# Decoder block on one core: score tiles split in two, and feed forward kept out of the weighted-values stages

## The chip, the cores and the metric

The kernel runs on one core of a Trainium2 chip. A core has a matrix engine (TensorE, PE in the profile, whose weight loads are listed as PEld), a vector engine (VectorE, DVE), an activation engine (ScalarE, ACT), a general engine (GpSimd, POOL) and a queue engine (SyncE, SP) that issues transfers here. Each engine takes its instructions in order. Two memories on the core matter: SBUF, which all engines read, and PSUM, eight banks of 128 partitions x 512 float32 numbers, into which TensorE writes. The metric is the device time of the one launch in microseconds, lower is better.

## The reference

Two sequences of 1024 tokens, 256 channels, 16 heads of 16 channels. Causal self attention, cross attention on a context of 77 tokens, and a gated feed forward with two hidden layers of 1024, each followed by a residual sum and a layer norm:

```python
x = _layernorm(x + attn(x, w_qkv, w_proj))            # causal, rotary, 16 heads
x = _layernorm(x + xattn(x, ctx, ctx, mask, Wq, ...)) # 77 keys
h = silu(x @ w1.T * w1_s) * (x @ w2.T * w2_s)
h = gelu(h @ h1.T * h1_s)
h = gelu(h @ h2.T * h2_s)
x = _layernorm(x + h @ w3.T * w3_s)
```

## The kernel before

The tokens are cut into five chunks (`CHUNKS`): two of 2 tiles of 128 tokens, then three of 4 tiles. For each chunk the attention work is a generator that goes through these stages:

- `start` (`project`): queries, keys and values, turned by the rotary tables.
- `top` (`maxima`): scores of each query tile against all keys that it sees, only to take the largest of each row. The scores of four heads stand in one PSUM tile `su` of four banks (`scores_bank`, L113), one head in each; one VectorE reduction (`part`, L432) takes the maxima of all four. The maxima are then added to the queries as a 17th row, so that later scores come out shifted.
- `weighted` (`values`, with `weights_and_values`): for each group of four heads and each key tile, TensorE writes the scores S into `su` (keys on partitions, up to 512 queries of four heads, 4 x 512 numbers for each partition), ScalarE takes the exponential into `pr` (L495), GpSimd clears what lies above the diagonal (L498), and TensorE sums the weighted values W of the step before into `po`.
- `rest` (`finish`, `cross`, `finish`): the division and projection, and the same for the cross attention, with its own maxima (`top`) and four steps of weighted values of 77 keys.

PSUM is full: `su` takes four banks and there is one such tile, `po` one, and three single banks serve everything else. So the scores of the next step cannot be written until the exponential (or the reduction) of this step has read all of `su`.

The feed forward of a chunk is a second generator (`fed`, `feed_forward_exact`). It works with bfloat16 products: each float32 operand is split into three bfloat16 parts, whose weights fit one bfloat16 exactly. It can begin once the attention of its chunk is done. `beside` (L861) weaves the two: each attention step yields a number of microseconds, its credit, and feed forward steps are drawn until the credit is spent. A step of the maxima yields 2.6 for 512 keys (L442), a step of weighted values 1.4 for 512 queries (L474), self and cross alike. From L940 on the engines keep the order of the program (`in_order`), so what is drawn at a yield stands on TensorE's queue between two attention steps. When the filler has run out or cannot go on, it yields nothing, and the attention steps stand alone; what is left of it after the attention is done runs by itself (L874). Attention runs in the order: `top(1)`, `weighted(1)`, then `rest(1)` woven with `start(2)` and `top(2)`, `weighted(2)`, and so on to `rest(4)`; the feed forward of the last chunk follows alone. Before all that, a first part without the fixed order does the attention of chunk 0 and surveys the weights (L820).

The functions that the change touches:

Of the kernel before, what the change touches and what calls it, by code (L numbers as in the profile page):

```python
# [9 lines left out]
F32 = mybir.dt.float32  # L10
# [28 lines left out]
def kernel(ctx: ExitStack, tc: tile.TileContext, a: dict, out: bass.AP):  # L39
# [73 lines left out]
    def scores_bank(name="su"):  # L113
        return pl.ps_u.tile([P, 4, 512], F32, tag="u", name=name)
# [205 lines left out]

    phase = [""]
# [75 lines left out]
    def maxima(b, t0, n, q):  # L397

        late = None
        for i in range(n):  # L400
# [3 lines left out]
            for m, (kk, c0, c1) in enumerate(spans):  # L404
                diagonal = m == len(spans) - 1
                r = c1 - c0
                gs = 512 // r
                for g0 in range(0, NG, gs):
                    gm = min(gs, NG - g0)
                    su = scores_bank()  # L410
                    calls = []
                    if diagonal:
                        for j in range(4):
                            to = su[:, j, :].rearrange("p (g n) -> p g n", g=NG)
                            mask = causal.unsqueeze(1).to_broadcast([P, NG, P])
                            calls.append(((to, ident_h, mask), dict(start=True, stop=False)))
                    for gi in range(gm):
                        for j in range(4):
                            rows = slice(32 * j, 32 * j + D)
                            calls.append(  # L420
                                (
                                    (
                                        su[:, j, gi * r : (gi + 1) * r],
                                        q[rows, g0 + gi, cols],
                                        kT[b, kk][rows, g0 + gi, c0:c1],
                                    ),
                                    dict(start=not diagonal, stop=(not diagonal or gi == gm - 1)),
                                )
                            )
                    tiled(calls)  # L430
                    turned = turned_maxima(m_pad) if late else None
                    dve.tensor_reduce(  # L432
                        part[:, m, g0 : g0 + gm, :].rearrange("p g j -> p j g"),
                        su[:, :, : gm * r].rearrange("p j (g r) -> p j g r", g=gm),
                        AX.X,
                        ALU.max,
                    )
                    if late:
                        add_maxima(turned, q, late)
                        late = None  # L440
                    phase[0] = "maxima"
                    yield 2.6 * gm * r / KB  # L442
# [7 lines left out]
    def weights_and_values(n, steps, q):  # L450
# [5 lines left out]
        def weigh(g, first, last, pr, heads, q0):  # L456
            if first:
                po[0] = pl.ps_o.tile([P, n * P], F32, tag="o", name="po")
            tiled(
                ((po[0][32 * j : 32 * j + 32, q0:], heads(j), pr[:, j, q0:]), dict(start=first, stop=last))  # L460
# [5 lines left out]
        for g, first, last, scores, weights, heads, q0 in steps:  # L466
# [7 lines left out]
            yield 1.4 * (n * P - q0) / KB  # L474
# [4 lines left out]
    def values(b, t0, n, q):  # L479
# [3 lines left out]
        def step(g, k):  # L483
# [3 lines left out]
            def scores(su):  # L487
                for j in range(4):
                    rows = slice(32 * j, 32 * j + D + 1)
                    key = kT[b, k // KT][rows, g, at * P : (at + 1) * P]  # L490
                    yield (su[:, j, q0 : n * P], key, q[rows, g, q0:]), dict(start=True, stop=True)

            def weights(su):
                pr = pl.probs.tile([P, 4, n * P], F32, tag="pr", name="pr")
                act.activation(pr[:, :, q0:], su[:, :, q0 : n * P], AF.Exp)  # L495
                if k >= t0:

                    nc.gpsimd.affine_select(  # L498
                        out=pr[:, :, q0 : q0 + P],
                        in_=pr[:, :, q0 : q0 + P],  # L500
                        compare_op=ALU.is_ge,
                        fill=0.0,
                        base=0,
                        pattern=[[0, 4], [1, P]],
                        channel_multiplier=-1,
                    )
# [7 lines left out]
        yield from weights_and_values(n, [step(g, k) for g in range(NG) for k in range(nk)], q)  # L514


    def cross(b, t0, n, qx):
# [8 lines left out]
        for i in range(n):  # L526
# [3 lines left out]
            for j in range(4):  # L530
                to = su[:, j, : NG * L].rearrange("p (g l) -> p g l", g=NG)
                mask = maskq[:, t0 + i, :].unsqueeze(1).to_broadcast([P, NG, L])
                calls.append(((to, ident_h, mask), dict(start=True, stop=False)))
            for g in range(NG):
                for j in range(4):
# [3 lines left out]
                            (su[:, j, g * L : (g + 1) * L], qx[rows, g, cols], kx[b][rows, g, :]),  # L539
# [6 lines left out]
            dve.tensor_reduce(  # L546
                top.rearrange("p g j -> p j g"),
                su[:, :, : NG * L].rearrange("p j (g l) -> p j g l", g=NG),
                AX.X,
                ALU.max,  # L550
            )
# [11 lines left out]
        def step(g):  # L563
            def scores(su):
                mask = maskk[:, t0 * P : (t0 + n) * P]
                for j in range(4):
                    yield (su[:L, j, : n * P], ident_h[:L, :L], mask), dict(start=True, stop=False)
                for j in range(4):
                    rows = slice(32 * j, 32 * j + D + 1)
                    yield (su[:L, j, : n * P], kx[b][rows, g, :], qx[rows, g, :]), dict(start=False, stop=True)  # L570

            def weights(su):
                pr = pl.probs.tile([P, 4, n * P], F32, tag="pr", name="pr")
                act.activation(pr[:L], su[:L, :, : n * P], AF.Exp)
                return pr[:L]
# [3 lines left out]
        yield from weights_and_values(n, [step(g) for g in range(NG)], qx)  # L579
# [281 lines left out]
    def beside(work, filler):  # L861
# [4 lines left out]
        for step in work:  # L866
            credit += step + stepped()
            while credit > 0:
                credit -= next(filler, None) or credit
            yield step  # L870
        attending[0] = False
# [64 lines left out]
    def beside_each_other(forward, wbufs):  # L936
        attended.clear()
# [103 lines left out]
```

## Time and profile before

| what | value |
|---|---|
| median of 3 runs | 1352.59 us (1347.74 to 1359.89) |
| the profiled execution | 1358.01 us, its span 1356.0 us |
| TensorE busy, mean granted clock | 1168.7 us, 0.861 |
| maxima, reduction of 4 x 512 numbers | 2291 ns each, 60 of the 76 |
| weighted values, exponential of 4 x 512 numbers | 1877 ns, 44 times |
| table loads of ScalarE | 27, 1283 ns each |

The stages lie in the span as follows, read from the first and last products of each tile: the first part to 143 us; `top(1)` to 179; `weighted(1)` to 217; `rest(1)`, `start(2)`, `top(2)` to 357; `weighted(2)` to 407; the same for chunk 3 to 644 and 763, for chunk 4 to 1009 and 1129; `rest(4)` to 1221; the last feed forward to the end.

A row of the busy time by stage gives the stretch in microseconds and its length, then for each engine the busy time and the number of instructions, then the granted clock of TensorE (1.00 is full speed), the share of the transfer engines and GB/s. A row of the timeline gives start, duration, engine, line, operation, the tile written and the tiles read, the shapes, and in brackets the idle time before it and what ended it. All attention and feed forward instructions are recorded through one helper, so their line is L81; they are told apart by their tiles: `su`, `pr`, `po` for attention, `pg`, `pu`, `pf` for feed forward. A float32 product counts as two instructions, so four heads are x8.

### The profile page before, as it was taken

What the parts mean: (1) busy time and instruction counts of PE and PEld (TensorE: products, weight loads), DVE (VectorE), ACT (ScalarE), POOL (GpSimd) and SP (SyncE); (2) the same over time, 40 slices, a digit from 0 to 9 for tenths busy, and PEclk for the clock granted to TensorE, in tenths of its full rate; (3) what the DMA queues carried; (4) which work ended last, traced back from release to release, by engine and by line L of the source; (5) the groups of instructions that cost most, each with busy time, mean ns of one, the idle gap of its engine ahead of it and who ended that gap; (6) DMA issues with size and microseconds to landing.
All of it is one profiled execution on the core that took longest, in us unless ns stands there. A gap on an engine that the chain in (4) does not pass through costs nothing.

```text
span 1356.0 us, 17661 instructions
## 1 busy us (share of the span) xinstructions
PE 1168.7 (86%) x7602; PEld 576.5 (43%) x7602; DVE 573.3 (42%) x868; ACT 395.6 (29%) x477; POOL 204.4 (15%) x262
## 2 busy tenths in 40 slices
PE   5878799987999768789898977788999988788997
PEld 3545456745546423334222454153332224433444
DVE  6442733436525434776212264157652024435112
ACT  4431243311352211112454320202134453223221
POOL 2010112111132100211202120002012021102221
PEclk7575899957999956899998996559998989969999
DMA  8740111110111000011000000000110000101110
GB/s 314 231 144 1 32 48 40 40 32 24 49 38 37 27 16 1 16 31 32 16 24 16 16 14 26 0 0 24 31 32 8 24 24 16 32 0 32 47 54 27
DMA packets 30952, 54.91 MB, mean 40 GB/s; under 512 B 5032, under 2 KB 10257, under 8 KB 30865
## 3 DMA queue, kind: packets, MB, share of 16 engines
q1 hardware_dynamic: 30593, 52.91, 12.6%
q8 instruction: 61, 1.00, 0.3%
q10 hardware_dynamic: 272, 0.79, 0.2%
q14 instruction: 26, 0.21, 0.0%
HBM read 45.82 MB, written 7.86 MB: 40 GB/s over the span
## 4 chain that ended last, share of the span: by engine, by line
PE 68%; DVE 18%; ACT 8%; POOL 2%; DMA 2%; issue 2%; SPq 0%; DVEq 0%; ACTq 0%; POOLq 0%
PE pf L81 24%; PE su L81 20%; PE pm L81 7%; DVE part L81 7%; PE po L81 6%; PE pt L81 5%; ACT pr L81 3%; DVE left L81 2%; PE pu L81 2%; PE pq L81 2%; DMA w<-in_wf_dram 2%; DVE gate L81 1%; DVE x L81 1%; PE pg L81 1%; DVE top L81 1%
## 5 line engine op out<-in xcount | busy, mean ns | idle before, releaser
L81 PEld LDWEIGHTS <-wf 128*128 128x128 bf16 x2400 | 224.3, 99 | 310.3 <-issue 150.5
L81 ACT ACTIVATE pr<-su 128x2048 f32<-128x2048 f32 (+3 forms) x124 | 171.2, 1381 | 231.9 <-PE su L81 230.2
L81 DVE TENSOR_REDUCE part<-su 128x4 f32<-128x2048 f32 (+3 forms) x76 | 165.6, 2179 | 85.9 <-PE su L81 85.4
L81 PE MATMUL pf<-mid,wf 128*128 128x512 bf16 (+1 forms) x640 | 171.2, 351 | 0.9 <-ACT v L81 0.7
L81 PE MATMUL pf<-hid,wf 128*128 128x512 bf16 (+1 forms) x640 | 166.7, 344 | 0.0
L81 PE MATMUL su<-q,kT 17*128 17x512 f32 (+3 forms) x832 | 101.0, 555 | 10.5 <-ACT pr L81 9.4
L81 PE MATMUL su<-kT,q 16*128 16x128 f32 (+3 forms) x1152 | 100.8, 463 | 8.1 <-DVE top L81 2.7
L81 PE MATMUL pf<-midm,wf 128*128 128x512 bf16 (+1 forms) x320 | 105.4, 342 | 1.2 <-ACT midm L81 1.1
L81 DVE COPY q<-po 128x512 f32<-128x512 f32 (+1 forms) x40 | 23.4, 585 | 195.0 <-PE po L81 195.0
L81 PE MATMUL pf<-hidm,wf 128*128 128x512 bf16 (+1 forms) x320 | 105.3, 337 | 0.0
L81 PE MATMUL po<-pr,v 128*32 128x512 f32 (+3 forms) x832 | 88.4, 500 | 14.7 <-POOL pr L498 14.6
L707 POOL TENSOR_TENSOR hid<-left 128x512 bf16<-128x512 f32 (+1 forms) x70 | 62.0, 891 | 215.4 <-DVE left L81 199.4
L498 POOL TENSOR_SCALAR_AFFINE_SELECT pr<-pr 128x512 f32<-128x512 f32 x64 | 42.6, 665 | 328.9 <-ACT pr L81 328.8
L81 ACT COPY hidm<-left 128x512 bf16<-128x512 bf16 (+1 forms) x70 | 36.3, 527 | 147.6 <-DVE left L81 147.6
L81 DVE TENSOR_TENSOR left<-hid 128x512 f32<-128x512 f32 (+1 forms) x80 | 51.6, 656 | 63.1 <-ACT hid L81 55.0
L81 PE MATMUL pu<-xTc,wf 128*128 128x512 bf16 (+1 forms) x160 | 50.9, 373 | 24.6 <-DVE gate L81 24.6
L81 PEld LDWEIGHTS su<-kT,q 16*128 16x128 f32 x1152 | 50.0, 219 | 45.1 <-issue 19.1
L81 PE MATMUL pg<-xTc,wf 128*128 128x512 bf16 (+1 forms) x160 | 51.7, 374 | 11.5 <-DVE q L81 7.5
L81 ACT ACT_TABLE_LOAD x27 | 34.6, 1283 | 88.2 <-PE su L81 87.9
L81 PEld LDWEIGHTS <-ident_h 128*128 128x128 bf16 (+1 forms) x208 | 26.4, 129 | 75.3 <-issue 67.1
L237 POOL TENSOR_SCALAR rstd<-mv 128x4 f32<-128x4 f32 (+1 forms) x15 | 3.4, 226 | 362.6 <-DVE mv L81 362.6
L81 PEld LDWEIGHTS su<-q,kT 17*128 17x128 f32 x832 | 35.8, 198 | 50.7 <-ACT pr L81 30.2
(125 smaller groups left out, 1403.4 us busy)
## 6 DMA issues: line engine op xcount, KB each, us to landing
wf<-wh SPq DMA_DIRECT2D x110, 256.0 KB, 2.6
w<-in_wf_dram SPq DMA_DIRECT2D x22, 512.0 KB, 5.5
wh<-h SPq DMA_DIRECT2D x22, 256.0 KB, 2.8
x<-in_x_dram SPq DMA_DIRECT2D x16, 128.0 KB, 3.1
out_dram<-x SPq DMA_DIRECT2D x16, 128.0 KB, 1.8
wqkv<-in_w_qkv_dram ACTq DMA_DIRECT2D x1, 768.0 KB, 4.4
wk<-in_wkT_dram SPq DMA_DIRECT2D x1, 512.0 KB, 7.3
wq<-in_wqT_dram SPq DMA_DIRECT2D x1, 512.0 KB, 4.9
```

The source lines that it names most:

```text
L81: ins = getattr(self.engine, name)(*args, **kw).ins
L237: nc.gpsimd.tensor_scalar(rstd, mv[:, :, 1], EPS, None, ALU.add)
L498: nc.gpsimd.affine_select(out=pr[:, :, q0 : q0 + P], in_=pr[:, :, q0 : q0 + P], compare_op=ALU.is_ge, fill=0.0, base=0, pattern=[[0, 4], [ ...
L707: nc.gpsimd.tensor_tensor(lower[:, k, :], left[:, 0, :], left_upper, ALU.subtract)
```

## The change

The scores of four heads become two tiles of two banks each, with a tag of their own, so each half is free on its own. For weighted values a new function `exponentials` lets VectorE copy the second half to SBUF while ScalarE takes the exponential of the first, then ScalarE takes that of the copy in place. The selection on GpSimd is done once for each half. For maxima a new function `largest` makes two reductions, one for each half; when feed forward has run out (`starving`), ScalarE first copies the second half to SBUF and the second reduction reads the copy. A step of weighted values of self attention yields 0.0 instead of 1.4, of cross attention 0.4; a step of the maxima yields 1.6 while starving and 2.6 otherwise. `beside` sets `starving` from what the filler answered.

```diff
     def scores_bank(name="su"):
-        return pl.ps_u.tile([P, 4, 512], F32, tag="u", name=name)
+        return [pl.ps_u.tile([P, 2, 512], F32, tag=f"u{i}", name=name) for i in range(2)]
...
+    def exponentials(su, p, cols):
+        n = cols.stop - cols.start
+        halves = [pl.probs.tile([P, 2, n], F32, tag=f"pr{i}", name=f"pr{i}")[:p] for i in range(2)]
+        dve.tensor_copy(halves[1], su[1][:p, :, cols])
+        act.activation(halves[0], su[0][:p, :, cols], AF.Exp)
+        act.activation(halves[1], halves[1], AF.Exp)
+        return halves
+
+    def largest(to, su, groups, r):
+        first, other = (t[:, :, : groups * r].rearrange("p j (g r) -> p j g r", g=groups) for t in su)
+        if starving[0]:
+            aside = pl.probs.tile([P, 2, KB], F32, tag="pr1", name="aside")[:, :, : groups * r]
+            aside = aside.rearrange("p j (g r) -> p j g r", g=groups)
+            act.copy(aside, other)
+            other = aside
+        dve.tensor_reduce(to[:, :2], first, AX.X, ALU.max)
+        dve.tensor_reduce(to[:, 2:], other, AX.X, ALU.max)
+
+    starving = [True]
...
-                    dve.tensor_reduce(
-                        part[:, m, g0 : g0 + gm, :].rearrange("p g j -> p j g"),
-                        su[:, :, : gm * r].rearrange("p j (g r) -> p j g r", g=gm),
-                        AX.X,
-                        ALU.max,
-                    )
+                    largest(part[:, m, g0 : g0 + gm, :].rearrange("p g j -> p j g"), su, gm, r)
...
-                    yield 2.6 * gm * r / KB
+                    yield (1.6 if starving[0] else 2.6) * gm * r / KB
...
-    def weights_and_values(n, steps, q):
+    def weights_and_values(n, steps, q, fill):
...
-            yield 1.4 * (n * P - q0) / KB
+            yield fill * (n * P - q0) / KB
...
-                pr = pl.probs.tile([P, 4, n * P], F32, tag="pr", name="pr")
-                act.activation(pr[:, :, q0:], su[:, :, q0 : n * P], AF.Exp)
+                pr = exponentials(su, P, slice(q0, n * P))
                 if k >= t0:
-                    nc.gpsimd.affine_select(
...
+                    for half in pr:
+                        nc.gpsimd.affine_select(
...
-        yield from weights_and_values(n, [step(g, k) for g in range(NG) for k in range(nk)], q)
+        yield from weights_and_values(n, [step(g, k) for g in range(NG) for k in range(nk)], q, 0.0)
...
-        yield from weights_and_values(n, [step(g) for g in range(NG)], qx)
+        yield from weights_and_values(n, [step(g) for g in range(NG)], qx, 0.4)
...
             while credit > 0:
-                credit -= next(filler, None) or credit
+                took = next(filler, None)
+                starving[0] = took is None
+                credit -= took or credit
             yield step
-        attending[0] = False
+        attending[0] = starving[0] = False
...
     def beside_each_other(forward, wbufs):
+        starving[0] = True
```

## The prediction

> **What bounds the kernel now.** I read the page first (engines, slices with the granted clock), then busy time by stage, then the groups with their shapes apart, then the order of time inside one step. TensorE is busy 1168.7 of 1356.0 us, but its granted clock is the second half of the story:
>
> ```profile
> PE 1168.7 (86%) x7602; PEld 576.5 (43%) x7602; DVE 573.3 (42%) x868; ACT 395.6 (29%) x477; POOL 204.4 (15%) x262
> PEclk7575899957999956899998996559998989969999
> ...
> core 0: us, PE busy (x) PEld busy (x) DVE busy (x) ACT busy (x) POOL busy (x), PEclk, DMA share, GB/s
> 179.00:217.00 38.00, 36.02 (x400) 19.96 (x400) 8.25 (x20) 20.67 (x22) 7.70 (x12) 1.00 0.15 41
> 287.00:309.00 22.00, 16.80 (x100) 10.79 (x98) 12.66 (x27) 0.75 (x2) 1.87 (x4) 0.50 0.11 34
> 357.00:407.00 50.00, 45.47 (x427) 22.88 (x426) 13.23 (x27) 27.04 (x22) 15.41 (x24) 0.97 0.13 39
> 407.00:466.00 59.00, 52.12 (x343) 36.23 (x341) 26.62 (x58) 15.70 (x31) 11.58 (x14) 1.00 0.11 32
> 466.00:546.00 80.00, 58.97 (x348) 27.13 (x347) 33.93 (x56) 10.26 (x9) 2.21 (x4) 0.64 0.04 10
> 644.00:763.00 119.00, 110.03 (x712) 32.77 (x710) 22.53 (x29) 58.77 (x38) 19.81 (x24) 0.94 0.07 18
> 821.00:910.00 89.00, 69.53 (x370) 33.09 (x369) 32.12 (x47) 10.95 (x10) 1.25 (x2) 0.53 0.02 5
> 1009.00:1129.00 120.00, 110.99 (x710) 32.55 (x709) 22.22 (x29) 58.77 (x38) 19.80 (x24) 0.93 0.06 18
> 1178.00:1204.00 26.00, 21.37 (x86) 5.07 (x87) 5.71 (x13) 8.77 (x5) 1.27 (x2) 0.62 0.12 37
> 1204.00:1221.00 17.00, 13.85 (x57) 9.31 (x56) 9.58 (x27) 1.49 (x4) 1.25 (x2) 0.80 0.00 0
> 1221.00:1356.00 135.00, 120.09 (x576) 55.63 (x574) 36.73 (x63) 32.95 (x51) 28.71 (x28) 0.97 0.13 40
> ```
>
> Weighted values are the rows at 179, 357, 644 and 1009 (327 us). The rows at 287, 466, 821, 1178 and 1204 (234 us) are stretches in which feed forward has run out: TensorE is busy about three quarters of them at nearly half clock. Now the inside of a step, and rows without feed forward:
>
> ```profile
> 706.17 1.14 PE L81 MATMUL su<-q,kT 17*128 17x512 f32 x8 [0.26 <-ACT pr L81]
> 707.24 1.06 PE L81 MATMUL po<-pr,v 128*32 128x512 f32 x8
> 707.44 1.88 ACT L81 ACTIVATE pr<-su 128x2048 f32<-128x2048 f32 x1 [1.32 <-PE su L81]
> 708.24 0.63 PE L81 MATMUL pf<-mid,wf 128*128 128x512 bf16 x2
> ...
> 885.00:905.00 20.00, 19.78 (x83) 12.69 (x84) 7.59 (x18) 1.49 (x4) 0.00 (x0) 0.50 0.00 1
> 1185.00:1203.00 18.00, 16.70 (x65) 3.20 (x64) 2.08 (x3) 5.62 (x3) 0.00 (x0) 0.50 0.03 8
> ```
>
> A step is scores (S), exponentials and the previous step's weighted values (W), with feed forward filling TensorE during the 1.88 us exponential. The last two rows have no feed forward: TensorE is busy 99% and 93% of them and stays at 0.50.
>
> **Where feed forward goes.** I counted its products between the stages in the instruction order of both programs, at 0.217 us for 512 columns (92 in each 20 us of 1260 to 1300). Total 458.3 us in both. The four stages of weighted values lose 15.4, 18.9, 43.0 and 43.0 and keep under 1 each. The stretches between gain 6.3 (217 to 357), 27.7 (407 to 644), 31.7 (763 to 1009) and 4.0 (1129 to 1204). What stands after the last attention work of the values kind grows from 114.6 to 162.7, so 48.1 of it is new there.
>
> **Weighted values, at full clock.** The scores tile is freed by halves: the exponential of a half is 1.02 us (the 128x1024 form, 1023 ns); a VectorE copy of 1024 numbers is not in the trace: at least 0.69 (512 numbers), and by the step from 425 ns (256) to 692 ns (512) it is 1.23, which I take as nearer in kind. Then S 1.14 and 0.19 of hand-over (0.06 from ScalarE to TensorE at 498.59, 0.13 back at 707.31): 2.56 us. W (1.00) lies beside the other exponential, and ScalarE's own 2 x 1.02 is under it. Narrower steps by the same sum: 2.1 (384), 1.6 (256), 1.5 for 128, where two selections on GpSimd take the place of one of 0.63. Each stage starts with a bare wait of 2.7 us: table load 1.28, exponential, hand-over, now with no product to cover it. A long stage has 20 full steps and 4 of each narrow width: 51 + 20.8 + 2.7 = 74.5; the stage at 357 has 4 full ones: 34; the one at 179 has 12 of 256 and 4 of 128: 28. Sum 211 against 327: -116.
>
> **Weighted values, at half clock.** Then TensorE's S and W bound the step: 2.00 and 1.94 in the cross steps at 1185 (matmul rows at 1185.31 and 1187.24), 3.94 in all. From the first stage of the program: 1.24 + 1.08 for 256, 0.81 + 0.66 for 128, 3.1 for 384 between them. 20 x 3.94 + 4 x (3.1 + 2.3 + 1.45) + 2.7 = 109; 46 and 36 for the shorter ones. Sum 300: -27 only, for 120 us of feed forward that has to be done elsewhere.
>
> Which clock? Every fall in the trace follows two to three microseconds with little TensorE work (the clock is 0.50 from 475 after a wait of 2.7 us). The start of each values stage now has such a wait, so I expect a fall in most. The way back is slow without feed forward: 46 to 73 is 26.50 of 27 us busy at 0.50, then it rises at 75. I take half of the stage at each clock: 255, **-72** (-116 to -27).
>
> [...]
>
> **The stretches between.** Starved work at full clock is busy time times clock: 8.4, 37.7, 36.9, 13.2 and 11.1 us. With filler TensorE is 88% busy (row at 407), so 9.5, 42.8, 41.9, 15.0, 12.6; plus the feed forward gained (6.3, 27.7, 31.7, 4.0 and some 8 in the last finish) that is 16, 70.5, 73.6 and 39.6 in place of 22, 80, 89 and 43: -34. But the four cross steps of a stage get only 0.4 of credit each; at half clock they cost 5.8 each (1185.31, 1191.18, 1197.03) instead of 2.9, 35 us over three long stages: 0. I take the middle, **-17**.
>
> **The end.** 48.1 less 8 is 40 us of feed forward alone, at 120.09 / 114.6 = 1.05: 42, and one layer boundary with no attention to cover gelu (1.91) and splitting: 5. **+47**. Nothing hides it.
>
> **Small terms.** Maxima now take two reductions: 1536 numbers take 1756 ns and 2048 take 2291, so 0.15 us more per pair. Some 50 pairs stand on VectorE in the stages; where filler covers them nothing, on the path 8; but the first half is free earlier, so perhaps a gain of 4: +3. Returning to feed forward at half clock, 4 x 1.5: +6 (0 to 12). ScalarE's aside copies appear twice in the branch that runs: nothing. First stage to 143 us, reordered by the scheduler: 0 (-5 to +8).
>
> **Sum.** 1356 - 72 - 17 + 47 + 9 = 1323 of span. The profiled run was 1358.0 at span 1356.0, the median 1352.6, so 3 off: **1319**.
>
> **Rivals.**
> Full clock in values and cross: -116 - 34 + 47 + 3 = -100, 1253. [...] Against: the bare 2.7 us at each start. Chance 0.17.
> Half clock throughout: -27 + 0 + 47 + 15 = +35, **1388**, slower. Place: TensorE's S and W in the values stages. It decides from the point where about three quarters of values and cross run at half clock (100 / 135). For it: the rows at 885 and 1185. Against: the rises at 75, 533 and 1208 without feed forward. Chance 0.25.
> The change does less than it says: if VectorE and ScalarE do not work side by side on the two tiles, a step is 1.02 + 1.23 + 1.14 + 0.19 = 3.6 at full clock, near the 3.5 of now but without filler: about 60 us over the full steps, 1375. They share no queue, so 0.05, within the slower case's bounds.
> The mixed case, my forecast: 0.53, itself 1285 to 1352.
>
> **How the numbers follow.** About 1% (13.5 us) is what a measurement tells from no change. Faster: the full-clock case and four fifths of the mixed one, 0.60; same: the upper end of the mixed and the low end of the half-clock one, 0.20; slower 0.20. Range 1258 to 1382, which leaves a tenth at each end.
>
> **What would show it.** In the after profile: clock in the values stages (0.5 or 1.0), a full step of 2.6 or 3.9 us, no stretch of 20 us without products of feed forward before the end, and some 160 us of feed forward alone at the end instead of 120. Wrong would be: starved stretches that remain, a step over 4 us, or maxima that lengthen although their filler is the same.

## The result, and the profile after

The changed kernel took 1405.9 us (median of 4 runs, 1400.99 to 1421.36) against 1350.16 us of the kernel before (4 runs beside it): a ratio of 1.042, 95% interval 1.032 to 1.053. It is slower; the forecast was 1319. The profiled execution took 1401.64 us, with a span of 1399.9 us.

First the page of the changed kernel: engines, the granted clock in 40 slices, and groups of instructions (busy us, mean ns, then idle time before).

```profile
PE 1240.9 (89%) x7602; PEld 589.0 (42%) x7602; DVE 663.9 (47%) x1044; ACT 429.0 (31%) x636; POOL 215.4 (15%) x326
PEclk8585889987899877998858997989955596999998
L81 PE MATMUL su<-q,kT 17*128 17x512 f32 (+3 forms) x832 | 151.7, 749 | 16.9 <-ACT pr L81 12.8
L81 PE MATMUL po<-pr,v 128*32 128x512 f32 (+3 forms) x832 | 146.0, 711 | 0.7
```

TensorE runs the same 7602 instructions and is busy for 72 us more. The two groups of the weighted values, scores and sums, on the page of the kernel before:

```profile
L81 PE MATMUL su<-q,kT 17*128 17x512 f32 (+3 forms) x832 | 101.0, 555 | 10.5 <-ACT pr L81 9.4
L81 PE MATMUL po<-pr,v 128*32 128x512 f32 (+3 forms) x832 | 88.4, 500 | 14.7 <-POOL pr L498 14.6
```

In the changed kernel they take 108 us more for the same products. The mean clock fell from 0.861 to 0.834, but that is only about half of it: in e16 below, where these stages run at 1.00, 0.87, 1.00 and 0.96, the two groups still take 124.7 and 115.3 us, 58 us less than here. The rest goes with the halves, whose products stand further apart: at full clock the scores of a full step spread over 1.58 us (678.58 below, clock 1.00 from 678 to 694), against 1.14 in the step at 706.17 of the kernel before (1.00 from 706 to 709). Busy time by stage of the changed kernel, columns as before:

```profile
core 0: us, PE busy (x) PEld busy (x) DVE busy (x) ACT busy (x) POOL busy (x), PEclk, DMA share, GB/s
181.00:211.00 30.00, 28.15 (x263) 12.15 (x261) 11.58 (x21) 17.89 (x33) 6.41 (x16) 0.78 0.04 10
...
355.00:394.00 39.00, 34.45 (x258) 10.84 (x257) 16.26 (x23) 24.13 (x34) 13.50 (x33) 0.82 0.03 8
...
476.00:507.00 31.00, 29.11 (x131) 9.71 (x130) 9.47 (x11) 12.29 (x12) 0.00 (x0) 0.61 0.06 17
507.00:552.00 45.00, 37.50 (x242) 24.35 (x240) 26.23 (x57) 7.63 (x17) 9.86 (x14) 0.82 0.16 47
...
649.00:746.00 97.00, 93.60 (x515) 23.06 (x515) 35.04 (x36) 55.69 (x64) 12.97 (x32) 0.64 0.00 1
1010.00:1119.00 109.00, 105.38 (x516) 24.07 (x517) 35.87 (x37) 58.24 (x67) 14.89 (x34) 0.52 0.00 1
...
1190.00:1400.00 210.00, 186.25 (x904) 90.22 (x902) 65.42 (x124) 43.13 (x65) 40.87 (x40) 0.96 0.14 41
```

The two long stages (649, 1010) are free of feed forward, 97% busy, and mostly at half clock (0.64 and 0.52 on average). Now the inside of their steps, from the timeline of the changed kernel: a step at full clock (1.00 from 678 to 694), the fall, and a step at half clock (0.50 from 1020 to 1104).

```profile
678.58 1.58 PE L81 MATMUL su<-q,kT 17*128 17x512 f32 x8
680.09 1.08 PE L81 MATMUL po<-pr,v 128*32 128x512 f32 x8
681.10 1.58 PE L81 MATMUL su<-q,kT 17*128 17x512 f32 x8
...
694.82 1.40 PE L81 MATMUL su<-q,kT 17*128 17x512 f32 x8 [0.81 <-ACT pr L81]
696.14 1.81 PE L81 MATMUL po<-pr,v 128*32 128x512 f32 x8
697.89 2.09 PE L81 MATMUL su<-q,kT 17*128 17x512 f32 x8
...
1020.30 2.09 PE L81 MATMUL su<-q,kT 17*128 17x512 f32 x8
1022.32 1.94 PE L81 MATMUL po<-pr,v 128*32 128x512 f32 x8
1022.49 1.02 ACT L81 ACTIVATE pr<-su 128x1024 f32<-128x1024 f32 x1 [1.50 <-PE su L81]
1022.55 1.23 DVE L81 COPY pr<-su 128x1024 f32<-128x1024 f32 x1 [2.66 <-PE su L81]
1023.81 1.06 ACT L81 ACTIVATE pr<-pr 128x1024 f32<-128x1024 f32 x1 [0.30 <-DVE pr L81]
1024.19 2.09 PE L81 MATMUL su<-q,kT 17*128 17x512 f32 x8
```

From scores to scores it is 2.52 us at full clock (678.58 to 681.10) and 3.89 at half (1020.30 to 1024.19). VectorE and ScalarE do start side by side (1022.49, 1022.55), and the copy takes 1.23 us: the split does what it says.

Where the time went, stage by stage, bounded by the first and last TensorE products of each stage as the timeline gives them (each column adds up to its span, within 0.1 us). `rest(4)` is counted here to its last weighted values of cross attention; the last finish, up to 1221 in the kernel before, is part of the end. The two columns on the right are experiments, explained below; they belong here because they split the loss in two.

| us | before | after | before, 32 rows | after, 32 rows |
|---|---|---|---|---|
| up to `weighted(1)` | 179.2 | 181.4 | 167.4 | 182.3 |
| the four values stages | 324.2 | 271.5 | 317.3 | 216.1 |
| the three stretches between | 625.5 | 664.9 | 606.0 | 649.9 |
| `rest(4)` | 74.9 | 71.1 | 74.2 | 69.7 |
| end | 152.2 | 211.0 | 152.5 | 209.4 |
| span | 1356.0 | 1399.9 | 1317.5 | 1327.5 |

So the change gave 53 us in the values and paid 39 in the stretches and 59 at the end.

### The profile page after: what moved, and what is told of

Its sections match the earlier page's. It is cut to its first block, busy times and chain, and to the rows that moved or that the text cites. A ratio compares the mean times of both kernels' runs of the same rounds, so it can differ in the third digit from the quotient of the medians.

```text
span 1399.9 us, 18249 instructions
## 1 busy us (share of the span) xinstructions
PE 1240.9 (89%) x7602; PEld 589.0 (42%) x7602; DVE 663.9 (47%) x1044; ACT 429.0 (31%) x636; POOL 215.4 (15%) x326
## 4 chain that ended last, share of the span: by engine, by line
PE 75%; DVE 13%; ACT 5%; DMA 3%; issue 2%; POOL 1%; SPq 0%; DVEq 0%; POOLq 0%; ACTq 0%
PE pf L81 26%; PE su L81 22%; PE po L81 11%; PE pm L81 6%; DVE part L81 5%; PE pt L81 4%; PE pu L81 2%; DMA w<-in_wf_dram 2%; PE pq L81 2%; ACT pr L81 2%; PE pg L81 2%; DVE left L81 2%; DVE gate L81 1%; DVE x L81 1%; DVE q L81 1%
## 5 line engine op out<-in xcount | busy, mean ns | idle before, releaser
L81 DVE COPY pr<-su 128x1024 f32<-128x1024 f32 (+3 forms) x124 | 113.4, 914 | 236.0 <-PE su L81 221.1
L81 DVE TENSOR_REDUCE part<-su 128x2 f32<-128x1024 f32 (+3 forms) x147 | 164.7, 1161 | 103.0 <-PE su L81 102.7
L81 PE MATMUL su<-q,kT 17*128 17x512 f32 (+3 forms) x832 | 151.7, 749 | 16.9 <-ACT pr L81 12.8
L81 PE MATMUL po<-pr,v 128*32 128x512 f32 (+3 forms) x832 | 146.0, 711 | 0.7
L81 ACT ACTIVATE pr<-su 128x1024 f32<-128x1024 f32 (+3 forms) x124 | 95.9, 773 | 140.1 <-PE su L81 138.2
L81 ACT ACTIVATE pr<-pr 128x1024 f32<-128x1024 f32 (+3 forms) x124 | 100.2, 808 | 38.8 <-DVE pr L81 35.6
L81 PEld LDWEIGHTS su<-q,kT 17*128 17x128 f32 x832 | 54.8, 262 | 125.9 <-ACT pr L81 111.4
L517 POOL TENSOR_SCALAR_AFFINE_SELECT pr<-pr 128x256 f32<-128x256 f32 x128 | 51.7, 407 | 302.8 <-ACT pr L81 290.1
L81 PEld LDWEIGHTS po<-pr,v 128*32 128x32 f32 x832 | 23.9, 130 | 95.5 <-issue 60.3
L719 POOL TENSOR_TENSOR mid<-left 128x512 bf16<-128x512 f32 (+1 forms) x38 | 35.8, 959 | 160.3 <-DVE left L81 160.3
```

Of the source, the lines that this page charges most:

```text
L81: ins = getattr(self.engine, name)(*args, **kw).ins
L517: nc.gpsimd.affine_select(out=half[:, :, :P], in_=half[:, :, :P], compare_op=ALU.is_ge, fill=0.0, base=0, pattern=[[0, 2], [1, P]], channe ...
L719: nc.gpsimd.tensor_tensor(lower[:, k, :], left[:, 0, :], left_upper, ALU.subtract)
```

## The experiments

None of these kernels changes a sum; where idle products are added, nothing reads their result. All ratios are to the kernel before, run on the same chip beside them; its median there lay between 1350.5 and 1357.9 us.

| run | edit | median us | ratio, 95% interval | mean clock |
|---|---|---|---|---|
| e1 | after, credit 1.4 / 1.4 | 1320.5 | 0.976 [0.971, 0.980] | 0.886 |
| e2 | before, credit 0.0 / 0.4 | 1409.0 | 1.041 [1.037, 1.046] | 0.831 |
| e3 | after + two idle products a step | 1347.5 | 0.990 [0.984, 0.996] | 0.905 |
| e4 | after, credit 0.5 / 0.5 | 1340.6 | 0.990 [0.987, 0.994] | 0.892 |
| e5 | e3, credit 0.0 / 1.4 | 1310.6 | 0.970 [0.965, 0.975] | 0.927 |
| e6 | after, table loaded early | 1388.4 | 1.030 [1.023, 1.036] | 0.844 |
| e7 | e1 + idle products where starved | 1312.0 | 0.968 [0.962, 0.974] | 0.921 |
| e8 | e1, maxima not divided | 1351.6 | 0.997 [0.994, 1.000] | 0.867 |
| e9 | e5 + e7 | 1318.2 | 0.975 [0.971, 0.979] | 0.932 |
| e10 | after, credit 0.5 / 1.4 | 1307.9 | 0.967 [0.963, 0.971] | 0.908 |
| e11 | after, credit 0.0 / 1.4 | 1360.7 | 1.007 [1.004, 1.010] | 0.858 |
| e12 | e10, table loaded early | 1306.1 | 0.965 [0.961, 0.969] | 0.909 |
| e13 | e5, idle products float32, 128 rows | 1329.4 | 0.983 [0.978, 0.988] | 0.935 |
| e14 | e5, idle products bfloat16, 17 rows | 1425.5 | 1.053 [1.047, 1.060] | 0.834 |
| e15 | e5, one idle product | 1321.6 | 0.974 [0.969, 0.979] | 0.903 |
| e16 | after, scores 32 rows high | 1325.3 | 0.978 [0.971, 0.986] | 0.920 |
| e17 | e12, scores 32 rows high | 1294.7 | 0.958 [0.951, 0.966] | 0.928 |
| e18 | before, scores 32 rows high | 1323.4 | 0.979 [0.974, 0.983] | 0.905 |

Credits are written self / cross: microseconds of feed forward for a step of 512 queries.

### The parts of the change, one at a time

e1 puts the credits back and keeps everything else. e2 takes the credits out of the kernel before (`fill` is 0.0 for self, 0.4 for cross), which keeps its one tile.

```diff
 e1, on after:
-    yield from weights_and_values(..., q, 0.0)
+    yield from weights_and_values(..., q, 1.4)
-    yield from weights_and_values(..., qx, 0.4)
+    yield from weights_and_values(..., qx, 1.4)
 e2, on before:
-            yield 1.4 * (n * P - q0) / KB
+            yield fill * (n * P - q0) / KB
```

> The changed kernel with the credit of a step of weighted values back at 1.4, so that feed forward fills these stages as before; the tiles stay split. Theory CLOCK (without bfloat16 products the weighted values run at half clock, which is the 108 us that the groups of S and W are longer): granted clock of the four values stages 0.93 or more, a long stage 105 to 120 us, whole 1335 to 1360. Rival SPLIT (the halves themselves cost: 124 more copies, two exponentials, two reductions): whole 1375 or more although the clock is back. Rival PLACE (feed forward costs more in the stretches between and behind the attention than in the values, whatever the clock): about 1350 too, so this run tells only SPLIT from the others.

> The kernel before with one edit: a step of weighted values yields 0.0 (self) and 0.4 (cross) instead of 1.4; one tile of four banks as before. CLOCK: values stages mostly at 0.50 to 0.65; a full step is S 2.0, exponential 1.88 and hand-over 0.2, 4.1 us, a little longer than the 3.9 of the split tiles, since S cannot begin during the exponential; values in sum 290 to 310, whole 1410 to 1440. SPLIT: 1340 to 1365. PLACE: 1395 to 1420.

e1 is 2.4% faster than before and e2 4.1% slower. Taking the feed forward out is the whole loss: 85 us with two tiles (1320.5 to 1405.9), 54 with one (1354.5 to 1409.0), and both end at the same time. What e1 gains is in the maxima, as e8 shows: e1 with the starved branch switched off and the credit always 2.6.

```diff
-        if starving[0]:
+        if False:
-                    yield (1.6 if starving[0] else 2.6) * gm * r / KB
+                    yield 2.6 * gm * r / KB
```

> The split tiles with all credits at 1.4, but maxima never divided between the engines: no copy aside on ScalarE, and always 2.6 of credit. What of the 34 us by which the split kernel with filler is faster than the kernel before comes from that. If from the division in starved stretches: 1338 to 1352. If from the two tiles being free one by one: 1318 to 1328.

e8 stands at 0.997 [0.994, 1.000]: with feed forward in its place the split of the tiles is worth 0.6 per cent at most. The 31 us between e8 and e1 come from dividing the maxima when feed forward has run out, with the lower credit that goes with it. The group on e1's page:

```profile
L81 ACT COPY aside<-su 128x1024 f32<-128x1024 f32 (+1 forms) x26 | 24.3, 934 | 111.2 <-PE su L81 111.2
```

Twenty-six copies, 0.93 us on average (20 of 1024 numbers, 1.01 us each, and 6 smaller ones of cross attention), let VectorE read the second half from SBUF while TensorE writes the next scores. Now the amount of filler: e4 gives 0.5 to both kinds of step, e10 0.5 / 1.4, e11 changes the cross credit alone.

> The changed kernel with a credit of 0.5 for each step of weighted values, self and cross: real feed forward products in place of the idle ones, about as many as TensorE has time for in a step of 2.56 us. CLOCK: values stages at 0.93 or more and 75 to 85 us for a long one, some 35 us of feed forward off the rest; whole 1270 to 1320, the fastest so far. PLACE: 1375 to 1395 (a third of the way back to before). SPLIT: 1380 or more.

> Split tiles, credit 0.5 for a step of self values and 1.4 for a cross step, no idle products: feed forward itself holds the clock. CLOCK: against 0.5 for both (1340.6 us) the cross steps leave the half clock, some 25 to 35 us: 1300 to 1318, as fast as the kernel with idle products or faster, since nothing idle is computed. If 0.5 is too little to hold the clock in the self values: 1318 to 1335.

> The changed kernel with one number put back: a cross step yields 1.4 instead of 0.4; self values stay at 0.0. It prices the cross steps alone. CLOCK: the three cross stretches leave the half clock as they did under the idle products (37 us there): 1365 to 1382. If the 37 us needed the self values at full clock too: 1385 to 1405.

The cross credit alone (e11) is worth 45 us of 1405.9, though its long values stages still take 107 and 97 us. In e10 they take 81 and 92 with 0.5 of feed forward in each step, and e10 is faster than e1, in which they carry 1.4 and take 122 and 114. Here a little filler in the values (1307.9 us) is better than none (1360.7) and better than much (1320.5).

### Is it the clock, the place of the feed forward, or the waits?

e3 puts two products into each step of weighted values that do nothing but keep TensorE at work; feed forward stays out, so if its place were what costs, e3 would be slower still. e5 adds the cross credit 1.4.

```diff
             tiled(scores(su))
+            if Engine.strict:
+                warm = bank("warm")
+                half = wqkv.bitcast(BF16).rearrange("p k (n two) -> p k n two", two=2)[:, 0, :, 1]
+                for i in range(2):
+                    matmul(warm, half[:, :P], half[:, P : P + 512], start=True, stop=True)
```

> The changed kernel with two bfloat16 products of 128x512 without use added to each step of weighted values (self and cross, in the part with the fixed order), written to a bank of their own; feed forward stands where the change put it. The products are 0.22 us each at full clock, less than the 0.5 us that TensorE waits in a step. CLOCK: the values stages rise from 0.52 to 0.82 to 0.93 or more, a full step from 3.9 to 2.6 us, the long stages from 97 and 109 to 75 to 85 us, the cross steps from 22 to 26 us a stage to 13 to 18; whole 1300 to 1340, below the kernel before although TensorE has more to do. PLACE or SPLIT: 1395 to 1425.

> The kernel with the idle products, and the credit of a cross step back at 1.4 (self stays 0.0). It asks what of the 27 us between that kernel (1347.5) and the split one with all credits (1320.5) is the half clock of the cross steps. CLOCK: the three stretches of cross steps, 22, 32 and 30 us with the idle products, fall to 16 to 22 with more feed forward inside, whole 1322 to 1336. PLACE (feed forward costs its full time wherever TensorE's chain of waits is not broken by it): 1340 to 1350.

More work, less time: e3 takes 58 us off the changed kernel and e5 95. The groups on e3's page:

```profile
L81 PE MATMUL su<-q,kT 17*128 17x512 f32 (+3 forms) x832 | 108.5, 547 | 10.4 <-ACT pr L81 5.6
L81 PE MATMUL po<-pr,v 128*32 128x512 f32 (+3 forms) x832 | 97.3, 500 | 0.6
...
L81 PE MATMUL warm<-wqkv 128*128 128x512 bf16 x189 | 65.4, 413 | 5.7 <-issue 5.7
```

The 65.4 us of idle products bring scores and values from 151.7 and 146.0 back to 108.5 and 97.3. e5 against e11, which differ by the idle products alone (mean clock 0.927 and 0.858), gives the price of the lower clock in the steps of weighted values, self and cross: 50 us, net of what the idle products take. Having feed forward stand elsewhere is no loss by itself: e5, at 1310.6, is no slower than e1 at 1320.5 (their intervals overlap).

The prediction held the wait at the start of each stage to be what brings the clock down. e6 was to take most of it away by loading ScalarE's table early:

```diff
         late, po = None, [None]
+        early = pl.small.tile([P, 1], F32, tag="early", name="early")
+        act.activation(early, minus_half[:, :1], AF.Exp)
```

> The changed kernel with one exponential of one number put ahead of the first scores of each stage of weighted values, so that ScalarE's table load of 1.28 us is over when the first scores are done: the bare wait at the start falls from 2.7 to about 1.4 us. If this wait is what drops the clock (my prediction), the values stages stay at full clock until a later gap: sum 225 to 255 instead of 275, whole 1350 to 1385. Rival: without bfloat16 products the clock falls anyway, at the narrow steps at the end of a group of heads, and does not come back: 1390 to 1410.

e6 gained 17 us, but not in the self values, and there it is no test of the wait. In the long stage, first of the changed kernel, then of e6, the wait after the first scores is 1.11 us in both, and the clock falls in both (0.51 from 652 to 673 in the changed kernel; in e6 the weighted values of 512 queries take 1.94 us, as at 0.50 above):

```profile
651.25 1.92 PE L81 MATMUL su<-q,kT 17*128 17x512 f32 x8 [1.11 <-ACT pr L81]
```

```profile
632.13 1.14 PE L81 MATMUL su<-q,kT 17*128 17x512 f32 x8
...
634.38 1.91 PE L81 MATMUL su<-q,kT 17*128 17x512 f32 x8 [1.11 <-ACT pr L81]
636.22 1.94 PE L81 MATMUL po<-pr,v 128*32 128x512 f32 x8
```

The four self stages of the changed kernel begin with waits of 0.68, 1.63, 1.11 and 1.24 us, not the 2.7 that the prediction put there, and those of e6 with 0.68, 1.71, 1.11 and 1.34. Its groups of scores and values take 153.3 and 147.4 us, no less than the changed kernel's. The gain is in two cross stretches, whose waits did shrink (1.68 and 1.89 us to 0.41 and 0.61) and which kept 1.00. So in these two a clock that held went with a shorter wait; whether the wait is what holds the long stages down is answered by e16 below, which has the same wait. e7 and e9 put idle products where feed forward has run out as well:

```diff
+                if took is None:
+                    held = bank("held")
...
+                    for _ in range(max(1, min(5, int(credit / 0.3)))):
+                        matmul(held, half[:, :P], half[:, P : P + 512], start=True, stop=True)
```

> The split tiles with all credits at 1.4 (1320.5 us), and where feed forward has run out, bfloat16 products without use: one to five of 128x512 each time that credit finds no filler. No work is moved. CLOCK: the starved stretches, at 0.5 to 0.75 in the slices of that run, rise to 0.9 or more and shorten by a quarter or more: whole 1265 to 1300. Rival WAITS (these stretches are bound by the chain through VectorE and ScalarE, not by TensorE's clock): 1312 to 1335, the idle products costing what the clock gives.

> The kernel with idle products in the values and cross credit 1.4 (1310.6 us), and also idle products wherever feed forward has run out. CLOCK: the short starved rests at the end of each chunk keep the clock, 1296 to 1308. WAITS: 1306 to 1318, no gain.

e7 is 8 us under e1 (mean clock 0.921 against 0.886), with intervals that overlap, and e9 no better than e5 (0.932 against 0.927): there the idle products seem to take about as long as they save.

### Which products hold the clock?

TensorE was 97% busy for 109 us at a clock of 0.52 (the row at 1010), so being busy did not keep the clock up there. The idle products that held it differ from the scores in two ways: bfloat16 against float32, and 128 rows against 17. e13 makes the idle products float32 and keeps 128 rows; e14 keeps bfloat16 with 17 rows; e15 halves the dose.

```diff
 e13, against e5:
-                    matmul(warm, half[:, :P], half[:, P : P + 512], start=True, stop=True)
+                    matmul(warm[:, :P], wqkv[:, 0, :P], wqkv[:, 0, P : 2 * P], start=True, stop=True)
 e14, in the same place:
+                    matmul(warm, half[: D + 1, :P], half[: D + 1, P : P + 512], start=True, stop=True)
 e15, against e5:
-                for i in range(2):
+                for i in range(1):
```

> The changed kernel with cross credit 1.4 and two idle products in every step of weighted values, as in the run of 1310.6 us, but the idle products are float32 (128 rows, 128 columns, one product as long as one of bfloat16 with 512 columns by the transposes at 415.77: 0.38 us for a product's two instructions) in place of bfloat16. The idle products' result is used by nothing. Theory 'kind': what holds the clock is bfloat16 work, float32 does not count; then the long self values stages are at half clock as without idle products, 107 and 98 us, and have some 18 us of idle products at half clock on top: about 1365 to 1400. Theory 'rows': what counts is how much of the array works, 128 rows against 17; then full-height float32 holds it as well, 1305 to 1320.

> The same kernel with the idle products in bfloat16, 512 columns, but with 17 rows only, the height of the scores. Theory 'kind': bfloat16 holds the clock, whatever its height: 1305 to 1320. Theory 'rows': a product of 17 rows does not count: the long stages at half clock, 1365 to 1400. If neither kind nor height is decisive but TensorE's share of busy time, both this run and the one with float32 stay at 1305 to 1320.

> The same kernel with one idle bfloat16 product of 128 rows in each step in place of two, 0.22 us in a step of 2.6 at full clock. If half the dose still holds the clock, the stages stay at full clock and lose up to 0.2 us for each of some 70 full steps: 1295 to 1310. If the clock needs a share of bfloat16 above a threshold between one product and two, it falls in at least one long stage: 1330 to 1365.

Busy time by stage of the two long values stages, first of e13, then of e14:

```profile
614.80:694.40 79.60, 77.98 (x641) 32.83 (x642) 34.58 (x35) 57.51 (x66) 13.07 (x32) 1.00 0.02 5
953.30:1035.00 81.70, 81.03 (x640) 33.98 (x642) 34.57 (x35) 57.36 (x65) 14.31 (x34) 0.96 0.00 1
```

```profile
626.80:756.00 129.20, 128.03 (x577) 31.76 (x578) 34.86 (x35) 57.79 (x66) 13.07 (x32) 0.52 0.01 3
1019.90:1149.00 129.10, 128.27 (x576) 31.95 (x578) 34.85 (x35) 57.61 (x66) 14.33 (x34) 0.51 0.00 1
```

What decides between these idle products is not the kind but the rows. With float32 of 128 rows the stages run at 1.00 and 0.96. With bfloat16 of 17 rows TensorE is 99% busy, so there are no waits left to blame, and the clock is 0.52 and 0.51. (e13's profiled execution, 1311.6 us at a mean clock of 0.935, was the fastest of its four; the others took 1326 to 1335 at 0.913 to 0.922 and were not profiled, so part of the stages may be at half clock in them.) The time of one product a step (e15) can't be told from that of two, as its interval overlaps that of e5, but its profile tells them apart: the two long stages have a clock of 0.88 and 0.79 (619.1 to 703.4 and 964.5 to 1054.8), those of e5 1.00 and 0.96.

If the rows make the difference, the scores themselves can be made taller without one product more. The four heads stand 32 rows apart, and the rows between hold zeros. e16 and e18 let the products run over all 32, in `maxima`, the values and the cross attention:

```diff
-                    rows = slice(32 * j, 32 * j + D + 1)
+                    rows = slice(32 * j, 32 * j + 32)
...
-                            rows = slice(32 * j, 32 * j + D)
+                            rows = slice(32 * j, 32 * j + 32)
```

> The changed kernel with all score products 32 rows high in place of 16 or 17. The rows added hold zeros in the queries (and zeros in the keys), so every sum is the same; the columns, and so the time of a product at a given clock, are the same. Theory 'height': the clock counts how many rows work, as the idle products of 128 rows (held it, float32 and bfloat16 alike) against those of 17 (did not) show; four heads side by side then use all 128 rows. If this is enough, the values stages come to full clock without feed forward: -50 us or more, 1300 to 1360. [...] Rival: the taller product takes longer (weights of 32 rows): slower than 1415, with S over 1.58 us at full clock.

e16 takes 1325.3 us: 80 off the changed kernel, with the same number of instructions, no idle product and no feed forward moved. Its values stages, by busy time:

```profile
182.30:208.80 26.50, 24.03 (x258) 11.18 (x258) 10.99 (x19) 17.49 (x33) 6.32 (x16) 1.00 0.04 11
346.90:384.10 37.20, 32.66 (x258) 10.50 (x258) 15.86 (x21) 24.23 (x34) 13.51 (x33) 0.87 0.03 9
633.10:708.40 75.30, 71.27 (x514) 22.63 (x514) 34.59 (x35) 54.15 (x64) 12.85 (x32) 1.00 0.00 1
971.20:1048.30 77.10, 72.92 (x513) 22.70 (x514) 34.59 (x35) 55.67 (x65) 14.06 (x34) 0.96 0.00 1
```

Full clock nearly throughout, with the waits left in place. Its timeline has the 1.11 us at the start of the long stage, and the very wait after which the changed kernel's clock fell at 694.82:

```profile
635.40 1.39 PE L81 MATMUL su<-q,kT 32*128 32x512 f32 x8 [1.11 <-ACT pr L81]
...
654.22 1.40 PE L81 MATMUL su<-q,kT 32*128 32x512 f32 x8 [0.81 <-ACT pr L81]
655.55 1.08 PE L81 MATMUL po<-pr,v 128*32 128x512 f32 x8
656.56 1.58 PE L81 MATMUL su<-q,kT 32*128 32x512 f32 x8
658.07 1.08 PE L81 MATMUL po<-pr,v 128*32 128x512 f32 x8
659.08 1.58 PE L81 MATMUL su<-q,kT 32*128 32x512 f32 x8
```

The same 0.81 us of waiting, and the next products take 1.08 and 1.58 us in place of 1.81 and 2.09. So the wait alone isn't what holds the long stages down. At full clock a taller product takes no more time: 1.58 us here as at 678.58 of the changed kernel. The cross steps of e16, however, whose scores are 32 rows high as well, stay at half clock without any gap:

```profile
470.00:490.00 20.00, 20.00 (x79) 4.97 (x77) 5.74 (x6) 7.68 (x9) 0.00 (x0) 0.50 0.02 6
```

Their masks and weighted values are 77 rows high and take half of that time (10.5 us).

> The kernel before, unchanged but for score products of 32 rows in place of 16 or 17 (zeros in the rows added, the same sums). It has feed forward between its steps of weighted values, but 234 us of starved stretches, most of them at half clock, made of maxima and cross attention. Theory 'height works everywhere': part of those stretches comes back to full clock, 1300 to 1340; then the changed kernel with 32 rows (1325.3) is no better than the kernel before with 32 rows, and taking feed forward out brings nothing by itself. Rival 'height decides in the values stages alone': before has full clock there already, so 32 rows give it nothing, 1345 to 1360; then with tall scores the change does what it was forecast to do, about -30 us.

e18 gives the kernel before 27 us as well, so the two stand level: 0.979 [0.974, 0.983] against 0.978 [0.971, 0.986]. They were not run side by side, and no difference between them is shown. With 32 rows in both, the change as made is worth nothing: the table of stages has -101 in the values, +44 in the stretches, -4 in `rest(4)`, +57 at the end and +15 ahead of `weighted(1)`. The stretches after `weighted(2)` and after `weighted(3)`, by busy time, first of e18, then of e16:

```profile
389.00:624.00 235.00, 196.16 (x1241) 97.51 (x1250) 131.06 (x173) 47.76 (x71) 29.40 (x32) 0.88 0.08 23
...
740.00:976.00 236.00, 197.76 (x1192) 96.25 (x1203) 134.03 (x175) 47.13 (x66) 29.39 (x28) 0.86 0.06 19
```

```profile
384.00:633.00 249.00, 221.54 (x1508) 119.71 (x1506) 143.45 (x219) 57.48 (x93) 34.74 (x40) 0.94 0.11 32
708.00:971.00 263.00, 226.32 (x1348) 105.24 (x1348) 150.22 (x224) 56.09 (x80) 37.55 (x35) 0.94 0.08 23
```

TensorE's busy time grows by 25 and 29 us, its idle time goes from 39 to 27 and from 38 to 37 (60 of e18's 7602 products are missing from its trace, so its busy time is a few microseconds too low). The feed forward that moved in lies mostly on the path, and little of it fills gaps.

### A version that beats both

e12 adds the early table to e10, e17 the 32 rows to e12.

> The best version so far (credit 0.5 in self values, 1.4 in cross values, 1307.9 us) with an exponential of one number ahead of each stage of weighted values, so that ScalarE loads its table before the scores stand. Theory 'table on the path': each of the eight stages (four self, four cross) gets back about 1.3 us of bare wait, and nothing else moves, so about 1298 us. Theory 'the wait brings the clock down': as in the changed kernel alone, where this edit gave 17 us because two cross stretches kept 1.00, some stage keeps its clock for longer and the time is 1290 or less. Rival 'covered': with feed forward between the steps TensorE has work during the table load, so it stays at 1304 to 1312.

> The fastest version so far (credit 0.5 in self values, 1.4 in cross values, early table load: 1306.1 us) with the same 32 rows. By 'height' the remaining stretches at half clock shrink: its mean granted clock of 0.909 rises, 1265 to 1295. [...]

e12 gains nothing that can be told from e10: in its self stages the wait after the first scores is 0.35 to 0.55 us with and without the early table, and three cross stages lose waits of 0.8 to 1.0 us. e17, with the two tiles, divided maxima, credits 0.5 / 1.4 and scores of 32 rows, is the fastest of all at 1294.7 us (1288.7 to 1300.8): 4.2% under the kernel before and 31 us under e16 on the same chip. Its gain over e12 is not certain, as the intervals overlap.

## Why the prediction was wrong

The profiled span is 1399.9 us, the forecast of it was 1323. Of the 77 us between, the values make 19, the stretches with `rest(4)` 52 and the end 12; the small terms, put at +9, are set against +2 ahead of `weighted(1)`. So two steps failed: the share of half clock, and, larger in size, the price of the stretches. The 1.5 us that the small terms hold for each of four returns to feed forward is shown by no run: in the changed kernel feed forward began at 0.50 behind three of the values stages and stayed there for 1.1, 2.1 and 1.9 us (from 210.60, 745.44 and 1117.74), and began at 1.00 behind the other (394.05). At half clock that costs about half of these 5.1 us, 2.5 by this estimate, in place of 6.

**Prices of the steps: right.** 2.56 us forecast for a full step at full clock, 2.52 measured; 3.94 at half clock, 3.89 measured; the copy 1.23, as taken between its bounds. At full clock the four stages were to take 211 us, and e16 has 216.1. Only the bare wait at each start, put at 2.7 us, was too long: it measured 0.68 to 1.63 us.

**"I take half of the stage at each clock: 255, -72": the step that failed first.** About three quarters of the values ran at half clock (198 to 212, 355 to 366, 379 to 383, 652 to 673, 697 to 748 and 1014 to 1119 by the clock in the stage rows and the length of the products), and they took 271.5 us, -53. Behind the share stood a wrong reading, "every fall in the trace follows two to three microseconds with little TensorE work". (Its own example, a wait of 2.7 us at 475, is 3.79 us in the trace, up to 475.95.) The kernel before already had a fall, at 372, with no wait over 0.92 us in the 7 us ahead of it, and in the changed kernel the clock fell at 652 after a wait of 1.11 us and at 198 with none over 0.39 us in the 7 us ahead. A wait may have been the occasion; the clock afterwards went with what ran. e14 removed nearly all waits and the long stages stayed at 0.52 and 0.51, and e16 kept the waits and they stayed at 1.00 and 0.96. The prediction had rows that warned of it, at 885 and 1185, 99% and 93% busy at 0.50, and gave them to a rival. What these two have in common is no feed forward, but not low products alone: at 1185 all products are 17 or 77 rows high, while at 885 products of 128 rows take 13.3 of the 19.8 busy microseconds, such as this one, and the rest have 16 rows or one:

```profile
898.62 1.91 PE L81 MATMUL pm<-wo,yT 128*128 128x256 f32 x4
```

Nor did the clock follow the busy share of TensorE: 129.2 us at 99% busy and 0.52 in e14, and 75.3 us at 95% busy and 1.00 in e16.

**"The stretches between", -17 forecast, +39 measured in the three and -4 in `rest(4)`: the step that failed by most.** The estimate let starved work shrink to its busy time at full clock once filler was there. Clock is not the reason that it failed, since with 32 rows it is +44. Some 66 us of feed forward were added by the counts of the prediction (6.3, 27.7 and 31.7), and two thirds of it came on top. In the rows of 507 to 552, feed forward joins the finish and the maxima; before, the same finish and maxima with hardly any of it took 29 us, after 45 us. Counted as the prediction counts it, feed forward there grows from 1.7 to 15.0 us: 13 us of filler cost 16. The row of the kernel before:

```profile
523.00:552.00 29.00, 23.11 (x124) 13.21 (x120) 18.42 (x34) 2.71 (x6) 3.69 (x4) 0.74 0.00 0
```

**The end, +47 forecast, +59 measured.** 48.1 us of feed forward at 1.05 is 50.5. The table's end holds the last finish as well, which was to take some 4 us more with the 8 us of feed forward put into it. Over this end TensorE's busy time grows from 134.2 to 187.4 us and its idle time from 18.0 to 23.7, so nothing of the feed forward went into gaps. The layer boundary left bare was to cost 5; on the changed kernel's timeline its longest wait is the first of these two. The second is for the layer norm of the last chunk, where the kernel before waits too, 3.15 us (at 1218.49):

```profile
1249.96 0.40 PE L81 MATMUL pf<-wf,hidm 128*128 128x256 bf16 x1 [2.16 <-ACT hidm L81]
...
1265.21 0.39 PE L81 MATMUL pg<-xTc,wf 128*128 128x512 bf16 x1 [4.23 <-DVE xTc L81]
```

**The rivals.** The slower one, half clock throughout at 1388, had the right mechanism and place, and a chance of 0.25; the measured time is 18 us above it (9 by the profiled spans), because the stretches, which it put at 0, cost 35 with `rest(4)`, and the end 12 more than it put there, while the values did better than it held. Its point of decision, three quarters at half clock, is where the kernel landed. The full-clock rival, 1253, would have failed too: e16 has its clock in the values and takes 1325, since the stretches and the end take back what the values give. That the split does less than it says is refuted by the timeline.

Open: why the part ahead of `weighted(1)` is 12 us shorter in e18 than in the kernel before while the same rows do nothing there for the changed kernel (its clock goes from 0.72 to 0.86 in the one and from 0.75 to 0.77 in the other); and why the rows make a difference (see the last section).

## What to carry to other kernels

Filler between short or narrow matrix products may be what keeps TensorE's clock up (here the two long values stages ran at 0.94 and 0.93 with it and at 0.64 and 0.52 without), so before taking it away, look in the trace for such products without filler and read the clock there; stretches like those at 885 and 1185 here, 99% and 93% busy at 0.50, are a warning. Where operands are padded with zeros anyway, run the product over the whole padded height: here going from 17 to 32 rows left the scores of a full step at 1.58 us at full clock, and gave 80 us in one kernel and 27 in the other. Read the clock again afterwards, since it did not rise in every stretch (0.50 at 470 of e16). And filler moved to a stretch that looks idle cost two thirds of its own time or more here.

## What was not expected of the hardware

In these runs the granted clock does not follow TensorE's busy time alone. Four scores of 17 rows side by side, 2.09 us, alternating with weighted values of 128 rows by 32 columns, 1.94 us, stay at 0.50 for 103 us with hardly a gap (98% busy from 1014 to 1117); with scores of 32 rows the two long stages of e16 are at 1.00 and 0.96. The rows added hold zeros, so in these steps a greater height named in the instruction was enough, with the same data. With two idle products of 128 rows in each step the long stages are at 1.00 and 0.96 as well, in float32 as in bfloat16 (e13, e5), and with two of 17 rows at 0.52 and 0.51 (e14). What heights between 17 and 32 rows do, and whether columns matter as well, was not tried. Nor does height go with the clock in every stretch: the row at 885 of the kernel before is at 0.50 with mostly 128 rows, the cross steps of e16 are at 0.50 with scores of 32 rows, and e18 still has 0.88 and 0.86 in the rows above. The clock also rose once without visible reason in a stretch of 17 rows, at 673 of the changed kernel (0.51 from 652 to 673, 0.99 from 673 to 697).
